# Key totals: a third accumulating fold to 16 rows, stacked half as wide, so that two squares a batch are turned and added in place of four

## The chip, the core and the metric

The kernel runs on one core of a Trainium2 chip. The core has five engines with a queue of instructions each: TensorE (PE in the profile, with its weight loads as PEld), VectorE (DVE), ScalarE (ACT), GpSimd (POOL) and SyncE (SP, which here only issues transfers). Each works through its queue in order, and engines wait for one another by semaphores. Transfers that SP and POOL issue are carried out by 16 DMA engines beside them. The metric is the time of one execution on the device in microseconds; lower is better.

## The reference

Input `x` has 32 images of 256 channels and 32 x 32 = 1024 positions. A group norm (32 groups of 8 channels) is followed by causal attention with eight heads of 32 channels, and `x` is added to the result. Cut to what matters here:

```python
q, k, v = heads(q_w @ xn + q_b), heads(kv_w @ xn + kv_b)      # 8 heads, 1024 positions, 32 channels
scores = q @ k.T / sqrt(32);  scores[query <= key] = -10000
attn = softmax(scores);       attn[query <= key] = 0
out = x + attn @ v
```

The softmax needs one total over the keys for each query. These totals, and how they are gathered, are what the change is about.

## The kernel before

**Layout.** A batch is one image. Scores are computed turned over: keys lie on the 128 partitions, queries along the rows. The exponentials of a block of scores are one tile `e` of 128 partitions x 4 heads x 512 queries, and TensorE multiplies it with `v` to the output `acc`. The total for a query is therefore a sum over partitions and over all tiles of keys. The kernel first adds the tiles to one another on VectorE (`add_keys`, line 469). What is left is called a square here: 128 partitions x 4 heads x 512 queries, four of them a batch (two groups `g` of four heads, two halves `hf` of the queries), numbered n = 0 to 3 in the code and called the first to the fourth.

**Loop.** The batches are cut into twelve visits each (`VISITS`, six for each group of heads). The loop at line 785 takes one visit after another, in this order: `scores` (products of queries and keys, exponentials on ScalarE, and on GpSimd in two visits of three the triangle mask of the blocks on the diagonal, `mask`, line 356), then the pieces of work that the dictionary `at` has for this visit, then `values` and `add_keys` of the visit before, then the pieces in `after`. All engines are scheduled by hand: what stands earlier in this order stands earlier in each engine's queue. `at` and `after` are filled at lines 739 to 784.

**From square to totals.** `fold(b, n, rows)` (line 478) has GpSimd issue an accumulating transfer that adds the partitions `rows` to `2 * rows` of a square to its first `rows` partitions. It runs with 64, then with 32; in front of the second square's second fold GpSimd drains. `stack` (line 484) has SyncE copy the 32 partitions that are left into the tile `folded`, each square at its own quarter of the partitions. When all four are there, `sum_folded` (line 490) goes through the four heads: VectorE turns 128 x 512 numbers in blocks of 32 x 32 and adds each row of 32, which leaves a query's total. `invert` takes the reciprocals, writes them to DRAM (line 536), and `spread_inverses` (line 545) reads them back to every channel's partition (`rb`); `finish` (line 568) multiplies, adds `x` and sends the result. The visits of a batch's folds are those of `SUMS = (3, 7, 10, 13)`, counted from the batch's first visit: those over 11 lie in the batch after.

**The group norm of the next batch** runs beside this. VectorE takes statistics (`norm_channels`), SyncE writes them to DRAM (`norm_gather`, line 198, tile `each`), GpSimd reads them back by groups (`norm_spread`, line 205, tile `eight`), VectorE aggregates them, GpSimd raises them to the power -1/2 and scales them (`norm_rstd`, lines 243 and 247, tiles `rstd` and `shift`), and ScalarE applies them (`norm_apply`, line 262, tile `xn`).

**The last batch** gets its totals from TensorE instead (`sums`, line 508, and `end_last`). It uses the same space: `rb_last` (line 557) and, in the very beginning, `less_mean` (line 706) lie in the tile tagged `folded`.

The lines that place the folds are these:

```python
v = first + SUMS[n]
late = int(n == 0)
when(v + 2 * late, lambda b=b, n=n: fold(b, n, 2 * HD), at if late else after)
when(v + 2 + late, lambda b=b, n=n: fold(b, n, HD), after)
when(v + 4, lambda b=b, n=n: stack(b, n), after if late else at)
```

Of the kernel before, what the change touches and what calls it, by code (L numbers as in the profile page):

```python
# [9 lines left out]
F32 = mybir.dt.float32  # L10
I32 = mybir.dt.int32
AF = mybir.ActivationFunctionType
ALU = mybir.AluOpType
# [4 lines left out]
P = 128  # L18
HD = 32
# [6 lines left out]
SUM_MAX = 1.0e20  # L26
HALFBANK = HALF // 2
ROW = 64
KEYS = 64


@with_exitstack
def tile_norm_attention_residual(
# [69 lines left out]
    def unshifted():  # L103
# [379 lines left out]

        def stack(b, n):
            if n == 0:
                live["folded", b] = work.tile([P, 4, HALF], F32, tag="folded", bufs=1, name=f"folded_{b}")
            total = live.pop(("sum", b, *divmod(n, NH)))
            nc.sync.dma_start(out=live["folded", b][n * HD : (n + 1) * HD], in_=total[:HD])

        def sum_folded(b, heads):  # L490
            if heads.start == 0:
                live["rows", b] = small.tile([P, ROW], F32, tag="rows", name=f"rows_{b}")
            for j in heads:
                turned = small.tile([P, HALF], F32, tag="turned", bufs=1, name=f"turned_{b}_{j}")
                nc.vector.transpose(turned, live["folded", b][:, j, :])
                nc.vector.tensor_reduce(
                    live["rows", b][:, j * HALF // HD : (j + 1) * HALF // HD],
                    turned.rearrange("p (k r) -> p k r", r=HD), AX.X, ALU.add,
                )

        def sum_keys(pd, e, of, start=True, stop=True):
            for j in range(4):
# [50 lines left out]
        def invert_here(b, n, within=slice(0, HALF)):  # L553


            if ("rb", b) not in live:
                live["rb", b] = work.tile([P, 4, HALF], F32, tag="folded", bufs=1, name="rb_last")
            k = (within.stop - within.start) // HD
            turned = small.tile([P, HALF], F32, tag="turned", bufs=1, name=f"turned_{b}_{n}_{within.start}")[:, : k * HD]
            nc.vector.transpose(turned, live["den", n][:, within])  # L560
            inv = inv_last[:, n, within.start // HD : within.stop // HD]
            nc.vector.reciprocal(inv, turned.rearrange("p (k r) -> p k r", r=HD)[:, :, 0])  # L562
            nc.vector.transpose(  # L563
                live["rb", b][:, n, within].rearrange("p (k r) -> p k r", r=HD),
                inv.unsqueeze(2).broadcast_to([P, k, HD]),
            )
# [124 lines left out]
        with tc.manual_schedule(engines={ENG.PE, ENG.Activation, ENG.DVE, ENG.Pool, ENG.SP}):  # L691
# [11 lines left out]
                norm_channels(0, g)  # L703
            norm_mean(0)
            keep_busy(2)
            odd = work.tile([P, 4, HALF], F32, tag="folded", bufs=1, name="less_mean")[:, 0, :]
            live["less_mean"] = odd.rearrange("p (g n t) -> p g n t", g=NG, t=P)
            for g in range(NG):
                nc.scalar.activation(
# [29 lines left out]
            for b in range(B):  # L739
# [14 lines left out]
                if not last:  # L754
                    for n in every:
                        v = first + SUMS[n]
                        late = int(n == 0)
                        when(v + 2 * late, lambda b=b, n=n: fold(b, n, 2 * HD), at if late else after)
                        when(v + 2 + late, lambda b=b, n=n: fold(b, n, HD), after)
                        when(v + 4, lambda b=b, n=n: stack(b, n), after if late else at)  # L760
                    late = b == B - 2
                    v = first + N + (5 if late else 6)
                    when(v, lambda b=b: sum_folded(b, every[:2]), after)
                    when(v + 1, lambda b=b: sum_folded(b, every[2:]), after)
                    when(v + 2, lambda b=b: invert(b))
                    for n in every:
                        at_visit = v + 2 + (0 if late else SPREAD[n])
                        if not late and n > 1:
                            when(at_visit, with_scores)
                        when(at_visit, lambda b=b, n=n: spread_inverses(b, n))  # L770
                    for n in every:
                        v = first + (N + 9 + n // 2 if late else FINISH[n])
                        later = None if late else lambda send, first=first, v=v, n=n: when(*((first + 2 * N + 4, send) if n < 2 else (v + 1, send, after)))
                        when(v, lambda b=b, n=n, later=later: finish(b, n, later=later), after)
                else:
                    when(first + 3, lambda: sums(0, SUMMED[1], False), after)
                    when(first + 7, lambda: sums(1, SUMMED[5], False), after)
                    when(first + 9, lambda: sums(2, SUMMED[7], False), after)
                    when(first + 8, lambda b=b: invert_here(b, 0))
                    when(first + 9, lambda b=b: finish(b, 0))  # L780
                    when(first + 8, lambda b=b: invert_here(b, 1))
                    when(first + 8, lambda b=b: finish(b, 1))
                    when(first + 10, lambda b=b: invert_here(b, 2))
                    when(first + 11, lambda b=b: finish(b, 2), after)
# [195 lines left out]
```

## Time and profile before

| what | value |
|---|---|
| time, median of 3 runs | 1791.73 us (1791.54 to 1792.0) |
| span of the profiled execution | 1791.2 us |
| PE busy | 1782.1 us, 99% |
| DVE busy | 1669.4 us, 93% |
| ACT busy | 1441.4 us, 80% |
| POOL busy | 897.9 us, 50% |
| mean busy share of the 16 DMA engines in the steady part | 0.70 |

The time of a run covers the span and what little lies around it; the profiled execution's own time isn't listed apart, and its span is 0.5 us below the median of the runs. The views used below are the page (totals of the span), the view by lines (groups of instructions of one kind, with their busy time, the mean of one, and the idle time before them), the view by windows (busy time of each engine in a stretch), the timeline of an engine (instructions in order of time, neighbours of one kind merged), and the view of DMA issues (size, and median time from issue to landing). A group's row reads: line, engine, operation, output <- inputs, shapes, count, then busy us and mean ns, then idle us of the engine before it and what ended that. Issuing a transfer from POOL counts as busy time of POOL, and the transfer itself goes on afterwards.

### The profile page before, as it was taken

The page shows a single profiled execution, that of the slowest core. Times are in us where ns is not written, and L with a number is a line of the kernel's source. Part 1 is how long each engine was busy: PE and PEld are TensorE (multiplying, and loading weights), DVE is VectorE, ACT ScalarE, POOL GpSimd, SP SyncE. Part 2 cuts the span into 40 slices and gives each one's busy share as a digit, 9 for nine tenths or more (in the row PEclk, how much of TensorE's full clock was granted, in tenths as well). Part 3 has the DMA queues.
Part 4 walks back from the last instruction along what each step waited for, and adds up shares of the span by engine and source line. Part 5 has one row for each costly group of instructions (what it writes and reads, how often), then busy time and mean ns, then how long its engine had stood idle before and what let it go on. Part 6 is the DMA issues. An engine that isn't in the chain of part 4 may idle for free.

```text
span 1791.2 us, 81784 instructions
## 1 busy us (share of the span) xinstructions
PE 1782.1 (99%) x37036; PEld 936.1 (52%) x37036; DVE 1669.4 (93%) x1796; ACT 1441.4 (80%) x1928; POOL 897.9 (50%) x935
## 2 busy tenths in 40 slices
PE   9999999999999999999999999999999999999998
PEld 5555555555555555555555555555555555555554
DVE  4689999999999999999999999999999999999998
ACT  6888878888778788788887888877888878888785
POOL 2355554554555555545555555454455554554542
PEclk9999999999999999999999999999999999999999
DMA  2567766767677676676776676767766766777663
GB/s 72 105 117 142 137 133 135 148 138 147 128 142 138 137 141 138 132 144 142 142 138 134 137 142 138 150 129 140 139 145 131 141 136 135 149 138 141 133 109 98
DMA packets 92771, 240.21 MB, mean 134 GB/s; under 512 B 26272, under 2 KB 27792, under 8 KB 76544
## 3 DMA queue, kind: packets, MB, share of 16 engines
q0 software_dynamic: 17360, 100.58, 40.1%
q1 hardware_dynamic: 74912, 134.28, 25.9%
q8 instruction: 290, 4.75, 1.1%
q14 instruction: 65, 0.53, 0.1%
q10 hardware_dynamic: 144, 0.07, 0.0%
HBM read 69.90 MB, written 34.95 MB: 59 GB/s over the span
## 4 chain that ended last, share of the span: by engine, by line
PE 99%; DVE 0%; ACT 0%; issue 0%; POOL 0%; POOLq 0%
PE sT L329 31%; PE acc L451 28%; PE pp L173 27%; PE ppv L173 13%; PE pd L503 1%; PE busy L159 0%; PE wt L152 0%; ACT e L426 0%; DVE rb_last L576 0%; DVE rb_last L563 0%; DVE turned L560 0%; DVE acc L573 0%; DVE inv_last L562 0%; POOL ident masks.py:199 0%; PE pv L173 0%
## 5 line engine op out<-in xcount | busy, mean ns | idle before, releaser
L426 ACT ACTIVATE e<-sT 128x1024 f32<-128x1024 f32 x768 | 744.3, 1022 | 301.5 <-PE sT L329 298.8
L366 POOL TENSOR_SCALAR_AFFINE_SELECT diagonal<-eh 128x512 f32<-128x512 f32 x512 | 563.3, 1122 | 625.4 <-ACT eh L422 624.7
L469 DVE TENSOR_TENSOR e<-e,e 128x1024 f32<-128x1024 f32 x314 | 578.0, 1841 | 23.0 <-ACT v L293 3.5
L329 PE MATMUL sT<-q,k 32*64 32x64 f32 (+1 forms) x18928 | 577.9, 367 | 0.1
L329 PEld LDWEIGHTS sT<-q,k 32*64 32x64 f32 x18928 | 397.0, 131 | 203.8 <-PE sT L329 67.4
L173 PE MATMUL pp<-xn,wT 128*32 128x512 f32 x4096 | 492.3, 598 | 0.0
L451 PE MATMUL acc<-e,v 128*32 128x512 f32 (+3 forms) x4608 | 401.0, 450 | 0.0
L422 ACT ACTIVATE eh<-sT 128x768 f32<-128x768 f32 (+1 forms) x384 | 341.6, 890 | 0.0
L451 PEld LDWEIGHTS acc<-e,v 128*32 128x32 f32 x4608 | 149.2, 110 | 261.5 <-issue 239.0
L173 PE MATMUL ppv<-wT,xn 128*32 128x256 f32 x4096 | 247.5, 382 | 0.0
L469 DVE TENSOR_TENSOR diagonal<-diagonal,e 128x1536 f32<-128x1536 f32 x126 | 194.5, 1544 | 16.1 <-PE acc L451 6.5
L173 PEld LDWEIGHTS pp<-xn,wT 128*32 128x32 f32 x4096 | 107.0, 109 | 195.8 <-issue 163.7
L469 DVE TENSOR_TENSOR e<-e,eh 128x1024 f32<-128x1024 f32 x126 | 177.6, 1410 | 6.5
L451 PEld LDWEIGHTS acc<-diagonal,v 128*32 128x32 f32 x4096 | 120.9, 110 | 88.1 <-issue 68.2
L173 PEld LDWEIGHTS ppv<-wT,xn 128*32 128x32 f32 x4096 | 120.2, 109 | 80.0 <-issue 7.0
L469 DVE TENSOR_TENSOR e<-e,diagonal 128x2048 f32<-128x2048 f32 x63 | 144.0, 2285 | 18.9 <-POOL diagonal L366 18.7
L451 PE MATMUL acc<-diagonal,v 128*32 128x128 f32 x4096 | 158.9, 273 | 0.0
L205 POOL DMA_INDIRECT eight<-each,group_of x31 | 42.9, 1383 | 193.4 <-DMA each<-st 193.4
L262 ACT ACTIVATE xn<-x,shift,rstd 128x256 f32<-128x256 f32 x248 | 137.2, 614 | 0.8 <-POOL shift L247 0.8
L576 DVE SCALAR_TENSOR_TENSOR rb<-num,v_bias_col,x 128x256 f32<-128x256 f32 x248 | 121.5, 530 | 4.4
L482 POOL DMA_DIRECT2D e<-e x124 | 103.6, 835 | 42.6 <-issue 42.6
L482 POOL DMA_DIRECT2D diagonal<-diagonal x124 | 105.1, 847 | 0.7
(87 smaller groups left out, 1092.2 us busy)
## 6 DMA issues: line engine op xcount, KB each, us to landing
x<-in_x_dram SPq DMA_DIRECT2D x124, 256.0 KB, 3.8
diagonal<-diagonal POOLq DMA_DIRECT2D x62, 512.0 KB, 6.1
e<-e POOLq DMA_DIRECT2D x62, 512.0 KB, 5.7
rb<-inverses SPq DMA_DIRECT2D x124, 256.0 KB, 4.0
out_dram<-rb SPq DMA_DIRECT2D x124, 256.0 KB, 4.2
diagonal<-diagonal POOLq DMA_DIRECT2D x62, 256.0 KB, 4.6
folded<-diagonal SPq DMA_DIRECT2D x62, 256.0 KB, 5.1
e<-e POOLq DMA_DIRECT2D x62, 256.0 KB, 4.6
```

Of the source, the lines that this page charges most:

```text
L173: nc.tensor.matmul(out[part], lhsT=lhsT[:, part], rhs=rhs, start=start, stop=stop, skip_group_check=True)
L205: nc.gpsimd.indirect_dma_start(eight, None, live["each", b].rearrange("(m c) s -> m (c s)", c=CPG), bass.IndirectOffsetOnAxis(ap=group_of[ ...
L262: nc.scalar.activation(to, of, AF.Identity, bias=live["shift", b][:, g : g + 1], scale=rstd)
L329: return nc.tensor.matmul(bank[c : c + KEYS, cols], lhsT=live["k", b, g][rows, kb * P + c : kb * P + c + KEYS], rhs=live["q", b, g][rows, ...
L366: nc.gpsimd.affine_select(out=square[:, :, place + s * P : place + (s + 1) * P], in_=raw[:, :, (1 - s) * KEYS : (3 - s) * KEYS], pattern=[ ...
L422: exp = nc.scalar.activation(eh.rearrange("p (n bank) q -> p bank n q", n=2)[:, :, :, :narrow], short[:, :, :, :narrow], AF.Exp)
L426: nc.scalar.activation(e[:, 2 * a : 2 * a + 2, :wide], pairs[a][:, :, :wide], AF.Exp)
L451: nc.tensor.matmul(acc[HD * j : HD * (j + 1), of], lhsT=live["v", b][:, kb, h * HD : (h + 1) * HD], rhs=e[:, j, :], start=first, stop=last ...
L469: nc.vector.tensor_add(to, to, tile_of(b, g, at))
L482: nc.gpsimd.dma_start(out=total[:rows], in_=total[rows : 2 * rows], accum_op=ALU.add)
L503: nc.tensor.matmul(pd[HD * j : HD * (j + 1), of], lhsT=pick, rhs=e[:, j, :], start=start, stop=stop, skip_group_check=True,)
L576: nc.vector.scalar_tensor_tensor(blocks(rb, s), blocks(num, s, (start + s) % 2 == 1), v_bias_col[:, g : g + 1], blocks(xt[:, g, cols], s), ...
```

## The change

The second fold is followed by a third, from 32 to 16 partitions (`TURN`), and each now comes one visit after the one before (with the first square one visit later than that, as before). `stack` copies 16 partitions in two halves of 256 queries, each half to 16 partitions of its own, so that `folded` has the same 128 partitions and half the columns. `sum_folded` turns two heads at once, 128 x 512 numbers, and adds rows of 16. The first square's `stack` comes one visit later. The tile is now tagged `stacked`; `rb_last` takes a slot of the pool of the images instead, and `less_mean` the narrower tile.

```diff
+TURN = 16
...
             if n == 0:
-                live["folded", b] = work.tile([P, 4, HALF], F32, tag="folded", bufs=1, name=f"folded_{b}")
+                live["folded", b] = work.tile([P, 4, HALFBANK], F32, tag="stacked", bufs=1, name=f"folded_{b}")
             total = live.pop(("sum", b, *divmod(n, NH)))
-            nc.sync.dma_start(out=live["folded", b][n * HD : (n + 1) * HD], in_=total[:HD])
+            for s in range(2):
+                at = n * HD + s * TURN
+                nc.sync.dma_start(
+                    out=live["folded", b][at : at + TURN], in_=total[:TURN, :, s * HALFBANK : (s + 1) * HALFBANK]
+                )
...
-            for j in heads:
-                turned = small.tile([P, HALF], F32, tag="turned", bufs=1, name=f"turned_{b}_{j}")
-                nc.vector.transpose(turned, live["folded", b][:, j, :])
-                nc.vector.tensor_reduce(
-                    live["rows", b][:, j * HALF // HD : (j + 1) * HALF // HD],
-                    turned.rearrange("p (k r) -> p k r", r=HD), AX.X, ALU.add,
-                )
+            turned = small.tile([P, HALF], F32, tag="turned", bufs=1, name=f"turned_{b}_{heads.start}")
+            nc.vector.transpose(turned, live["folded", b][:, heads.start : heads.stop, :].rearrange("p j q -> p (j q)"))
+            nc.vector.tensor_reduce(
+                live["rows", b].rearrange("p (j s k) -> p j k s", s=2, k=HALFBANK // HD)[:, heads.start : heads.stop],
+                turned.rearrange("p (j k s r) -> p j k s r", j=len(heads), s=2, r=TURN), AX.X, ALU.add,
+            )
...
-                live["rb", b] = work.tile([P, 4, HALF], F32, tag="folded", bufs=1, name="rb_last")
+                live["rb", b] = xpool.tile([P, NG, S], F32, tag="x", name="rb_last").rearrange("p g (hf q) -> p (g hf) q", hf=NH)
...
                         when(v + 2 * late, lambda b=b, n=n: fold(b, n, 2 * HD), at if late else after)
-                        when(v + 2 + late, lambda b=b, n=n: fold(b, n, HD), after)
-                        when(v + 4, lambda b=b, n=n: stack(b, n), after if late else at)
+                        when(v + 1 + 2 * late, lambda b=b, n=n: fold(b, n, HD), after)
+                        when(v + 2 + 2 * late, lambda b=b, n=n: fold(b, n, TURN), after)
+                        when(v + 4 + late, lambda b=b, n=n: stack(b, n), after if late else at)
```

## What was predicted

> **What bounds the kernel now.** The page comes first: span, busy line, granted clock.
>
> ```profile
> span 1791.2 us, 81784 instructions
> PE 1782.1 (99%) x37036; PEld 936.1 (52%) x37036; DVE 1669.4 (93%) x1796; ACT 1441.4 (80%) x1928; POOL 897.9 (50%) x935
> PEclk9999999999999999999999999999999999999999
> ```
>
> PE is never idle and has the full clock. DVE, the engine that the change relieves, is second at 93%. Whether PE's pace depends on DVE is read from three batches in the view by windows (columns: stretch, its length, then busy us of PE, PEld, DVE, ACT, POOL, then clock, DMA share, GB/s).
>
> ```profile
> 70.35:125.33 54.98, 54.98 (x1161) 28.86 (x1159) 45.41 (x43) 44.99 (x61) 26.12 (x30) 1.00 0.60 110
> 125.33:180.31 54.98, 54.98 (x1161) 28.86 (x1159) 51.61 (x56) 44.94 (x61) 26.81 (x29) 1.00 0.70 139
> 845.00:899.98 54.98, 54.98 (x1166) 28.86 (x1155) 52.70 (x57) 44.94 (x60) 28.55 (x29) 1.00 0.70 139
> ```
>
> The batch takes 54.98 us with 45.41 us of DVE work in it and with 52.70. DVE has nothing to give to the end time. What is left to ask is whether the change makes somebody else late for PE, and by the edit that is POOL, whose queue carries the accumulating transfers. Here is POOL's timeline for one steady batch (start, duration, engine, line, operation, tiles, and in brackets what it idled for). L366 is the triangle mask that PE's value products read, L482 an accumulating transfer, L205 the gather of the group norm of the batch after, L243 its power.
>
> ```profile
> 842.24 0.85 POOL L482 DMA_DIRECT2D diagonal<-diagonal  x1
> 848.16 2.24 POOL L366 TENSOR_SCALAR_AFFINE_SELECT diagonal<-eh 128x512 f32<-128x512 f32 x2 [5.07 <-ACT eh L422]
> ...
> 850.39 0.80 POOL L482 DMA_DIRECT2D diagonal<-diagonal  x1
> 852.75 1.66 POOL L366 TENSOR_SCALAR_AFFINE_SELECT diagonal<-eh 128x512 f32<-128x512 f32 x2 [1.56 <-ACT eh L422]
> 854.37 0.84 POOL L482 DMA_DIRECT2D e<-e  x1
> 861.49 1.28 POOL L205 DMA_INDIRECT eight<-each,group_of  x1 [6.29 <-DMA each<-st]
> 862.78 2.37 POOL L366 TENSOR_SCALAR_AFFINE_SELECT diagonal<-eh 128x512 f32<-128x512 f32 x2
> 865.11 0.85 POOL L482 DMA_DIRECT2D e<-e  x1
> 866.46 1.22 POOL L366 TENSOR_SCALAR_AFFINE_SELECT diagonal<-eh 128x512 f32<-128x512 f32 x2 [0.50 <-ACT eh L422]
> 867.85 2.69 POOL L243 TENSOR_TENSOR rstd<-rstd,power 128x2 f32<-128x2 f32 x1 [0.18 <-DVE rstd L217]
> ...
> 870.84 0.91 POOL L482 DMA_DIRECT2D diagonal<-diagonal  x1
> ...
> 878.68 0.82 POOL L482 DMA_DIRECT2D diagonal<-diagonal  x1
> ...
> 881.78 0.84 POOL L482 DMA_DIRECT2D e<-e  x1
> 888.98 2.81 POOL L366 TENSOR_SCALAR_AFFINE_SELECT diagonal<-eh 128x512 f32<-128x512 f32 x2 [6.36 <-ACT eh L422]
> 893.13 0.82 POOL L482 DMA_DIRECT2D e<-e  x1 [1.33 <-issue]
> 893.97 3.29 POOL L366 TENSOR_SCALAR_AFFINE_SELECT diagonal<-eh 128x512 f32<-128x512 f32 x2
> 897.21 0.85 POOL L482 DMA_DIRECT2D diagonal<-diagonal  x1
> ```
>
> Two things are to be seen. No transfer here waits for the one before it to land: the second fold of a square comes 7.8 us or more after the first. And the queue is in order: the gather idles 6.29 us for its input, and the mask behind it starts only at 862.78, when the gather is done. PE reads that mask, and the one of 888.98, here:
>
> ```profile
> 866.55 0.62 PE L451 MATMUL acc<-diagonal,v 128*32 128x128 f32 x16
> ...
> 894.04 0.62 PE L451 MATMUL acc<-diagonal,v 128*32 128x128 f32 x16
> ```
>
> The first mask ends at 865.15, so it has 1.4 us in hand; the second at 891.79, 2.2 us in hand.
>
> **The change, part by part.** DVE's part, from the view by line and shape:
>
> ```profile
> L495 DVE STREAM_TRANSPOSE turned<-folded 128x512 f32<-128x512 f32 x124 | 87.8, 708 | 2.2
> L496 DVE TENSOR_REDUCE rows<-turned 128x16 f32<-128x512 f32 x124 | 85.0, 686 | 4.3
> ```
>
> A batch loses four transposes and four sums, 4 x (0.708 + 0.686) = 5.6 us, and gets two of each, over the same 512 columns: 2.8 us. DVE goes from 52.7 to about 49.9 us of 54.98. A sum with 32 outputs in a four-step pattern isn't in the trace: I take 0.69 us, and at twice that DVE still does less than now. Worth to the span: 0, by the windows above. The one stall of PE that DVE causes in the whole trace bounds the gain: a DVE sum that took 2.50 us for its usual 1.41 (rows of the DVE and PE timelines), and later a block of scores of 2.25 us that is elsewhere 1.55.
>
> ```profile
> 605.06 2.50 DVE L469 TENSOR_TENSOR e<-e,eh 128x1024 f32<-128x1024 f32 x1
> ...
> 618.82 2.25 PE L329 MATMUL sT<-q,k 32*64 32x256 f32 x48
> ```
>
> That costs PE 0.7 us, once. The new places of `rb_last` and `less_mean` cost nothing: the slot in `xpool` was batch 28's, long finished, and the other is a smaller tile of the same lifetime.
>
> The transfers are what matters. A square gets a third fold, so POOL issues 12 a batch, not 8 (4 x 0.84 = 3.4 us more of a half idle engine: hidden if nothing waits). But the folds now follow each other one visit apart, 54.98 / 12 = 4.58 us, and each reads what the last one wrote. How long they take to land is in the DMA view (KB, us from issue to landing):
>
> ```profile
> diagonal<-diagonal POOLq DMA_DIRECT2D x62, 512.0 KB, 6.1
> e<-e POOLq DMA_DIRECT2D x62, 512.0 KB, 5.7
> diagonal<-diagonal POOLq DMA_DIRECT2D x62, 256.0 KB, 4.6
> ...
> e<-e POOLq DMA_DIRECT2D x62, 256.0 KB, 4.6
> ...
> each<-st SPq DMA_DIRECT2D x31, 12.0 KB, 5.3
> ```
>
> 6.1, 5.7 and 4.6 us are over 4.58: nearly every second and third fold will stop POOL's queue until the one before has landed, with masks, gather and power behind it (the first square's second fold keeps its old distance and waits only when the queue is late already). SP's queue has the same: `stack` of the third square stands ahead of the statistics that the gather waits for.
>
> ```profile
> 855.26 0.51 SPq L488 DMA_DIRECT2D folded<-diagonal  x1
> 855.87 1.56 SPq L198 DMA_DIRECT2D each<-st  x1
> ```
>
> It is issued when the last fold has landed (850.39 + 4.6 = 855.0 now), and is two issues instead of one. The 16-row fold isn't in the trace. From 512 to 256 KB the landing falls by 1.1 to 1.5 us, so another 128 KB less should take 0.55 to 0.75 off 4.6: I take 4.0 us. Its bounds are 4.6 us and, by the fastest `stack`, 2.9 us:
>
> ```profile
> DMA to landing us min/median/max: 2.9/4.9/7.0
> ```
>
> The waits now close into a ring, once round per batch, each step being queued behind or reading the one before. From the first fold of the third square: it lands 6.1; second fold lands 4.6; third 4.0; two stack issues 1.0; statistics land 5.3; gather 0.3 after that (861.49 against 855.87 + 5.3) and 1.3 long; mask 2.24; fold 0.85; mask 2.24; power and shift to the next transfer 3.0 (870.84 less 867.85); first square 6.1 and 4.6; its third issue 0.84; second square 5.7 and 4.6; its third issue 0.84; mask 2.24; and the third square is due again. The 2.24 is twice the mean of one select:
>
> ```profile
> L366 POOL TENSOR_SCALAR_AFFINE_SELECT diagonal<-eh 128x512 f32<-128x512 f32 x512 | 563.3, 1122 | 625.4 <-ACT eh L422 624.7
> ```
>
> The sum is 55.85 us. PE's batch is 54.98, so POOL's ring is 0.87 us longer and becomes the period. Followed by the clock it says the same: third fold at 842.24 + 10.7 = 852.9, landed 856.9, statistics issued at 858.0 instead of 855.87, so the mask of 862.78 starts 2.1 us late and has 1.4 us in hand: PE stalls 0.7 us. The ring is complete in batches 1 to 30, 30 times: 30 x 0.87 = 26 us. From the span, 1791.2 + 26 = 1817.2; the runs' median is 0.5 above the span, so **1817.7 us**.
>
> The drain ahead of the second square's second fold (the 1.33 us before 893.13) moves under the wait for the landing: 0.
>
> [...]
>
> **Bounds of the unknowns.** The 16-row fold: -1.1 to +0.6 us. Masks range from 1.22 to 3.29 us in the rows above, so the ring's three make -3.1 to +3.2. The second square's first fold (881.78) now takes 7.9 us:
>
> ```profile
> DMA to landing us min/median/max: 7.9/7.9/7.9
> ```
>
> Issued 2.3 us later, clear of most of the x loads, I take the median 5.7; up to +2.2 if not. Below a ring of 54.98 nothing happens; with masks at mean and 7.9 it is 58.05, 3.1 us a batch.
>
> **The rivals.**
> No change. The ring closes inside 54.98, for which 0.9 us of the three masks is enough (one as short as the 1.22 us row), and the masks' own 1.4 and 2.2 us in hand take the rest. DVE's 2.8 us of extra idle time per batch speaks for it, the in-order gather row and the 0.87 us against it. Time: 1791.7, give or take 1.5. This is the side on which the forecast would be wrong. If the change doesn't do what it says (a reduction as slow as the two it replaces), DVE's share comes out as before, and by the windows the time is the same as in this case.
> Much slower. The second square's fold still takes 7.9 us, POOL's shift comes late for ACT's normalisation too, and the ring is 3.1 us over: 1791.7 + 92 = 1884. For it: four transfers in flight around that moment. Against: their order changes.
> Faster. DVE would have to be on PE's path somewhere. It was once, for 0.7 us: 1791.0. A gain above 0.2% (3.6 us, about what a measurement of this kernel can tell from no change) has no place in the trace.
>
> **Chances.** Stall of some tenths to 2.5 us a batch, the forecast: 0.53. No change: 0.33. Much slower: 0.12. Faster by over 0.2%: 0.02. So faster 0.02, same 0.33, slower 0.65. The range goes from 1789 (no change at its lower end) to 1868 (2.5 us a batch, half way between the median ring and the long one with a little over), which leaves out most of the much slower case.
>
> **What would show it.** Right: in the windows of a batch, 55.3 to 57.5 us for the same 1160 or so matmuls; POOL's second and third folds with idle time before them, ended by a DMA; waits of PE or its loads for the masks; statistics issued some 2 us later within the batch. DVE at about 50 us a batch either way. Wrong: batches of 54.98 us with POOL waiting on landings all the same (then the masks had enough in hand), or folds that land within 4.58 us and don't wait. If batches are long but PE's blocks wait for ACT or DVE, the place is wrong and only the sign right.

## The result, and the profile after

The changed kernel takes 1968.16 us (median of four runs, 1966.90 to 1974.57) beside 1791.87 us for the kernel before in the same session (1791.54 to 1794.06): ratio 1.0989, with a 95% interval of 1.0972 to 1.1007. It is slower by 176.3 us, or 5.9 us for each of 30 batches. The forecast had the sign and the place, and was 150 us short. An experiment without a range below was timed once; repeated runs of the kernel before lie within 0.4% of one another.

All line numbers move up a little: the fold is L483 now, the mask L367, the gather L206, power L244, `stack` L491, the transposes L499 and the sums L500. From the page: span, busy times, and the shares of the chain of work that ended last.

```profile
span 1965.4 us, 82254 instructions
PE 1861.8 (95%) x37036; PEld 938.3 (48%) x37036; DVE 1595.1 (81%) x1672; ACT 1440.3 (73%) x1928; POOL 877.7 (45%) x1059
...
DMA 35%; PE 18%; POOL 16%; issue 13%; DVE 11%; ACT 5%; SPq 0%; POOLq 0%; DVEq 0%; ACTq 0%
```

PE, which was idle for 9 us, is now idle for 104, and a third of the chain is transfers that somebody waits for. PE's busy time has also grown by 80 us, with the same 37036 matmuls: at most 29 of these are a lowered clock (last section), and where the others come from was not followed up. No other engine has become busier to speak of; the rest is waiting. The view of waits names them (engine, tile and line, what was waited for: us in all, times, longest):

```profile
POOL diagonal L483 <- DMA diagonal<-diagonal: 352.2, 99, 6.9
POOL e L483 <- DMA e<-e: 280.5, 83, 6.8
...
POOL e L483 <- issue: 231.1, 33, 8.3
DVE e L470 <- POOL diagonal L367: 200.7, 32, 8.3
PEld acc L452 <- POOL diagonal L367: 158.9, 153, 3.9
POOL diagonal L367 <- ACT eh L423: 122.8, 44, 9.0
...
PE acc L452 <- POOL diagonal L367: 80.5, 90, 3.0
```

GpSimd spends 352.2 + 280.5 us before a fold, until the transfer before has landed. The 231.1 us of "issue" are the drain ahead of the second square's second fold (experiment `e3_no_drain` shows that). The idle time that GpSimd had before, 624.7 us of waiting for ScalarE's exponentials ahead of a mask, has shrunk to 122.8: its slack is used up, and now DVE, PE and PE's loads wait for the masks. One stretch of GpSimd's timeline has it in order:

```profile
890.20 0.92 POOL L483 DMA_DIRECT2D diagonal<-diagonal  x1 [0.33 <-PE sT L330]
893.60 4.15 POOL L367 TENSOR_SCALAR_AFFINE_SELECT diagonal<-eh 128x512 f32<-128x512 f32 x2 [2.48 <-ACT eh L423]
...
897.74 0.83 POOL L483 DMA_DIRECT2D diagonal<-diagonal  x1
898.29 1.52 POOL L367 TENSOR_SCALAR_AFFINE_SELECT diagonal<-eh 128x512 f32<-128x512 f32 x2
902.64 0.81 POOL L483 DMA_DIRECT2D diagonal<-diagonal  x1 [2.83 <-DMA diagonal<-diagonal]
903.25 1.06 POOL L483 DMA_DIRECT2D e<-e  x1
912.50 0.76 POOL L483 DMA_DIRECT2D e<-e  x1 [8.19 <-issue]
913.02 1.48 POOL L367 TENSOR_SCALAR_AFFINE_SELECT diagonal<-eh 128x512 f32<-128x512 f32 x2
917.84 0.81 POOL L483 DMA_DIRECT2D e<-e  x1 [3.33 <-DMA e<-e]
```

The first square's third fold (902.64) idles 2.83 us for its second. The second square's first fold is issued at 903.25, its second only at 912.50 after 8.19 us of idle time, and behind that stands the mask of 913.02. PE's timeline shows who needs it:

```profile
910.75 1.04 PE L452 MATMUL acc<-e,v 128*32 128x512 f32 x8
913.98 0.43 PE L452 MATMUL acc<-diagonal,v 128*32 128x128 f32 x8 [2.19 <-POOL diagonal L367]
```

The view of DMA issues (KB each, median us to landing) gives the sizes that the forecast had to estimate:

```profile
diagonal<-diagonal POOLq DMA_DIRECT2D x62, 512.0 KB, 6.5
e<-e POOLq DMA_DIRECT2D x62, 512.0 KB, 7.0
...
diagonal<-diagonal POOLq DMA_DIRECT2D x62, 256.0 KB, 4.7
e<-e POOLq DMA_DIRECT2D x62, 256.0 KB, 5.0
diagonal<-diagonal POOLq DMA_DIRECT2D x62, 128.0 KB, 4.2
...
e<-e POOLq DMA_DIRECT2D x62, 128.0 KB, 4.2
```

The forecast's ring can be measured link by link: the mean time from one of GpSimd's transfers (or the power) to the next, worked out from the trace over 22 steady batches, with the mean landing time of the first of the two beside it. In the kernel before the same count gives a period of 55.02 us.

```
link in GpSimd's queue (after)                  us   lands after
3rd square, first fold  -> second              6.67   6.37
3rd square, second fold -> third               5.01   4.70
3rd, third fold -> 4th square, first           1.73   4.14
4th square, first fold  -> second              6.36   6.08
4th square, second fold -> gather              1.60
gather -> 4th square, third fold               3.88
4th, third fold -> power                       3.30
power -> 1st square, first fold                3.31
1st square, first fold  -> second              7.67   7.14
1st square, second fold -> third               5.15   4.89
1st, third fold -> 2nd square, first           0.61   4.20
2nd square, first fold  -> second (drain)      8.71   7.67
2nd square, second fold -> third               5.26   4.96
2nd, third fold -> 3rd square, first           1.70   4.15
period                                        60.96
```

60.96 is 5.98 us over PE's 54.98; 30 of those are 179 us, against 176.3 measured. In 6 of the 14 links the next step comes about 0.3 us after a landing (1.04 behind the drain): these end in waits for a landing. Together they last 37.2 us of the 61. A seventh, the first square's first fold, has landed 0.5 us before the next step, which in most batches starts when the masks ahead of it end.

The ring is not closed by GpSimd alone. Between the gather and the power it runs through the gather's landing (5.6 us by the view of DMA issues, 3.0 before) and VectorE's aggregation, and the power waits for that in every batch:

```profile
DVE mv L213 <- DMA eight<-each,group_of: 81.9, 24, 5.0
...
POOL rstd L244 <- DVE rstd L218: 34.8, 31, 2.4
```

### The profile page after: what moved, and what is told of

Read it like the earlier page. It is cut to its first block, busy times and chain, and to the rows that moved or that the text cites. A ratio compares the mean times of both kernels' runs of the same rounds, so it can differ in the third digit from the quotient of the medians.

```text
span 1965.4 us, 82254 instructions
## 1 busy us (share of the span) xinstructions
PE 1861.8 (95%) x37036; PEld 938.3 (48%) x37036; DVE 1595.1 (81%) x1672; ACT 1440.3 (73%) x1928; POOL 877.7 (45%) x1059
## 4 chain that ended last, share of the span: by engine, by line
DMA 35%; PE 18%; POOL 16%; issue 13%; DVE 11%; ACT 5%; SPq 0%; POOLq 0%; DVEq 0%; ACTq 0%
DMA e<-e 19%; POOL diagonal L367 9%; DMA eight<-each,group_of 7%; PE sT L330 6%; DMA diagonal<-diagonal 6%; PE acc L452 5%; DVE e L470 4%; POOL rstd L244 4%; PE pp L174 4%; ACT e L427 3%; PE ppv L174 3%; DMA each<-st 2%; POOL diagonal L483 2%; DVE mv L213 2%; DVE st L190 1%
## 5 line engine op out<-in xcount | busy, mean ns | idle before, releaser
L330 PE MATMUL sT<-q,k 32*64 32x64 f32 (+1 forms) x18928 | 612.1, 375 | 3.8 <-ACT e L427 3.3
L367 POOL TENSOR_SCALAR_AFFINE_SELECT diagonal<-eh 128x512 f32<-128x512 f32 x512 | 481.0, 1047 | 123.0 <-ACT eh L423 122.8
L330 PEld LDWEIGHTS sT<-q,k 32*64 32x64 f32 x18928 | 411.6, 133 | 219.2 <-PE sT L330 61.0
L483 POOL DMA_DIRECT2D e<-e x186 | 167.7, 902 | 512.0 <-DMA e<-e 280.5
L483 POOL DMA_DIRECT2D diagonal<-diagonal x186 | 164.7, 886 | 362.2 <-DMA diagonal<-diagonal 352.2
L452 PE MATMUL acc<-diagonal,v 128*32 128x128 f32 x4096 | 178.2, 280 | 91.1 <-POOL diagonal L367 80.5
L174 PE MATMUL ppv<-wT,xn 128*32 128x256 f32 x4096 | 254.7, 389 | 0.0
L452 PEld LDWEIGHTS acc<-diagonal,v 128*32 128x32 f32 x4096 | 108.5, 110 | 222.8 <-POOL diagonal L367 158.9
L470 DVE TENSOR_TENSOR e<-e,eh 128x1024 f32<-128x1024 f32 x126 | 201.7, 1601 | 6.5
L244 POOL TENSOR_TENSOR rstd<-rstd,power 128x2 f32<-128x2 f32 x32 | 82.4, 2574 | 41.7 <-DVE rstd L218 34.8
```

The source lines that it names most:

```text
L174: nc.tensor.matmul(out[part], lhsT=lhsT[:, part], rhs=rhs, start=start, stop=stop, skip_group_check=True)
L244: nc.gpsimd.tensor_tensor(rstd, rstd, power, ALU.pow)
L330: return nc.tensor.matmul(bank[c : c + KEYS, cols], lhsT=live["k", b, g][rows, kb * P + c : kb * P + c + KEYS], rhs=live["q", b, g][rows, ...
L367: nc.gpsimd.affine_select(out=square[:, :, place + s * P : place + (s + 1) * P], in_=raw[:, :, (1 - s) * KEYS : (3 - s) * KEYS], pattern=[ ...
L452: nc.tensor.matmul(acc[HD * j : HD * (j + 1), of], lhsT=live["v", b][:, kb, h * HD : (h + 1) * HD], rhs=e[:, j, :], start=first, stop=last ...
L470: nc.vector.tensor_add(to, to, tile_of(b, g, at))
```

## The experiments

The theory to be tested: the period is set by GpSimd's queue, since each third fold waits there for the second one's landing, and the second for the first's. The rivals: the load of four more transfers a batch; the closer spacing alone; the drain; the path through `stack` and the statistics; and some cost of the narrower stack itself.

**The narrower stack and DVE's relief alone** (`e8_half_stack_alone`). The third fold is left out and the other folds and `stack` stand where they stood before, so each total lacks its partitions 16 to 31.

```diff
-                        when(v + 1 + 2 * late, lambda b=b, n=n: fold(b, n, HD), after)
-                        when(v + 2 + 2 * late, lambda b=b, n=n: fold(b, n, TURN), after)
-                        when(v + 4 + late, lambda b=b, n=n: stack(b, n), after if late else at)
+                        when(v + 2 + late, lambda b=b, n=n: fold(b, n, HD), after)
+                        when(v + 4, lambda b=b, n=n: stack(b, n), after if late else at)
```

> The changed kernel without the third fold, the first two folds and the stack at the visits of before. It leaves out half of each total (rows 16 to 31 of each square), so what is added up is not complete; stack in two halves, half as many squares turned and added, are as in the change. Theory (VectorE is off PE's path, eight small stack issues for four large ones are hidden): 1790 to 1793 us with VectorE some 2.8 us a batch less busy. Rival (the two halves of a stack cost SP or the DMA engines what PE then waits for): 1800 us or more. Rival (VectorE's relief is worth something that the third folds hide): under 1788 us.

It took 1792.00 us (1790.86 to 1792.66), ratio 0.9994, interval 0.9984 to 1.0004. A batch in the view by windows (busy us of PE, PEld, DVE, ACT, POOL):

```profile
845.00:899.98 54.98, 54.93 (x1158) 28.59 (x1149) 48.02 (x52) 44.83 (x60) 29.51 (x29) 1.00 0.64 123
```

DVE has the relief, and the batch still takes 54.98 us. What the change was to bring is worth nothing here, and the two half stacks cost nothing: all 176 us belong to the folds.

**The closer spacing alone** (`e1_spacing_only`): the kernel before, its second fold one visit after the first.

```diff
-                        when(v + 2 + late, lambda b=b, n=n: fold(b, n, HD), after)
+                        when(v + 1 + 2 * late, lambda b=b, n=n: fold(b, n, HD), after)
```

> The kernel before, with one edit: each square's second fold comes one visit after its first, as in the change. No third fold, no half-wide stack. Theory (a ring of waits on landings in GpSimd's in-order queue, closed once per batch): without the third folds the ring of the changed kernel loses 4.2 us (third square's landing), 4.9 + 0.6 less 1.9 us (first square), 5.3 + 0.5 + 1.2 less 3.5 us (second square) and some 1.4 us of the second stack issue, about 47 us in all, under 54.98, so it doesn't set the period; what can still be late is the mask behind the second square's second fold, by 0 to 0.5 us a batch: 1792 to 1806 us. Rival (the second folds' shorter distance is the harm, the third fold is only more of the same): at least half of the loss, 1875 us or more. Rival (the loss is DMA contention or the half-wide stack, not any wait in the queue): 1791 to 1793 us.

1807.20 us, 15 us more than before (1792.10) and 1 us past the upper end. Its waits:

```profile
POOL e L482 <- DMA e<-e: 395.7, 62, 10.4
...
POOL diagonal L482 <- DMA diagonal<-diagonal: 166.3, 31, 6.9
```

562 us of waiting on landings cost 15: two folds a square in a row still fit into GpSimd's slack, nearly.

**The third fold, with the first two at their old distance** (`e2_third_only`).

```diff
-                        when(v + 1 + 2 * late, lambda b=b, n=n: fold(b, n, HD), after)
-                        when(v + 2 + 2 * late, lambda b=b, n=n: fold(b, n, TURN), after)
+                        when(v + 2 + late, lambda b=b, n=n: fold(b, n, HD), after)
+                        when(v + 3 + late, lambda b=b, n=n: fold(b, n, TURN), after)
```

> The changed kernel with the first two folds of each square at the visits of before, and the third fold one visit after the second. Stack, turning and adding as in the change. Theory (ring of waits): the second folds no longer wait, the third ones still do, since a second fold takes 4.6 to 5.3 us and a visit is 4.58: the third square's third fold stands ahead of the fourth square's first one and of the stack that the statistics wait behind, and the fourth square's third fold stands ahead of the power. Mask after the gather late by some 2 us, shift late by 3 us: 2 to 4 us a batch, 1850 to 1910 us. Rival (only the shortened distance of the second folds matters): 1791 to 1800 us. Rival (contention and smaller packets of the added transfers, wherever they are placed): 1940 us or more.

1933.09 us: above the range. Only 35 us come back, though GpSimd waits far less for landings, 306 us in place of 633:

```profile
POOL e L483 <- DMA e<-e: 153.8, 58, 3.8
POOL diagonal L483 <- DMA diagonal<-diagonal: 152.5, 72, 3.4
```

So the sum of GpSimd's waits doesn't price them (562 us cost 15 in `e1_spacing_only`). What counts, by the theory, is whether the ring still closes in time: counted as above, it takes 59.7 us here. Which of its links made it longer than expected was not worked out.

**The same transfers without the wait** (`e9_third_aside`), the test that decides between wait and load. The third fold is issued at its place, with its 128 KB (as 32 rows of 4 KB, where the change has 16 rows of 8 KB), but adds a tile of zeros to itself, which nobody reads. The addition of partitions 16 to 31 is left out; `stack`, too, then waits for the second fold only.

```diff
+    aside = const.tile([P, 4, HALFBANK], F32, name="aside")
+    nc.gpsimd.memset(aside[: 2 * HD], 0.0)
...
+            if rows == TURN:
+                total, rows = aside, HD
```

> The changed kernel, its third folds at their places in GpSimd's queue, but adding 128 KB of a tile of zeros to itself (32 rows of 4 KB), so that they don't read what the second fold writes and have nothing to wait for. It leaves out the third sixteen rows' addition of each total. Transfers, bytes, stacks, VectorE work and queue order are those of the change. Theory (what costs is the queue standing still until the second fold has landed): the ring is open, what is left is what the shorter distance of the second folds costs (1807 us measured without third folds): 1800 to 1825 us. Rival (12 accumulating transfers a batch load the DMA engines or GpSimd so much that all land late): 1930 us or more. Between the two, the share of each.

1809.88 us, as expected. Its waits, and its row of the third folds in the view of DMA issues:

```profile
POOL e L487 <- issue: 239.8, 40, 8.8
POOL diagonal L369 <- ACT eh L425: 228.7, 119, 8.5
POOL diagonal L487 <- DMA diagonal<-diagonal: 180.7, 31, 6.6
POOL e L487 <- DMA e<-e: 163.4, 32, 7.6
```

```profile
aside<-aside POOLq DMA_DIRECT2D x124, 128.0 KB, 4.9
```

As many transfers of as many bytes in the same order, and 158 us of the 176 are gone. The second folds still wait for landings (180.7 and 163.4), and the drain is as long as ever; together with the added transfers they account for no more than the 17 us that are left. The earlier start of the stacks isn't what helps: in the changed kernel no engine waits for a stack to land, and the statistics, which queue behind the third square's stack, go ahead of it in `e5_stack_behind` (below) without any gain. The period of the ring, counted as above, is 55.6 us.

**The same at the places of `e2_third_only`** (`e10_third_aside_old_places`): the edit of `e9_third_aside`, with the same addition left out, and the two lines of `e2_third_only`.

> As the run before it, with the second folds at the visits of the kernel before, two visits after the first, and the third folds (of the zeros, leaving out the same part) one visit after those, as in the run with the third fold alone, which took 1933 us. Theory: nothing in GpSimd's queue waits for a landing any more: 1790 to 1796 us with the same 12 transfers a batch. Rival (the load of the transfers): 1900 us or more.

1811.24 us (1808.72 to 1813.48), ratio 1.0099, interval 1.0082 to 1.0116: the forecast of no change is missed by 15 us. So four more transfers a batch do cost something, about 1%, without anybody waiting for them; whether by their load on the DMA engines or by the time that GpSimd needs to issue them was not separated. Landings:

```profile
diagonal<-diagonal POOLq DMA_DIRECT2D x62, 512.0 KB, 6.8
e<-e POOLq DMA_DIRECT2D x62, 512.0 KB, 7.4
```

The first folds land at 6.8 and 7.4 us, in place of 6.1 and 5.7 before. Against `e2_third_only`, which has the same places and the wait, it is 122 us less: again the wait is the bulk. With `e9_third_aside` the parts are not additive: closer spacing alone is 15 us, the four transfers alone 19, both together 17.

**The drain** (`e3_no_drain`).

```diff
-            if (n, rows) == (1, HD):
-                nc.gpsimd.drain()
```

> The changed kernel without the drain of GpSimd ahead of the second square's second fold. Its trace has that fold starting 1.07 us after its predecessor's landing, where other folds start 0.28 us after. Theory (ring of waits, with the drain as one of its links): 0.8 us a batch less, 24 us, 1944 us (1935 to 1953). Rival (the drain is what makes the queue wait for landings, as its length of 8.8 us in the trace could suggest): the loss falls by half or more, under 1880 us. Rival (the drain is outside whatever sets the period): 1965 to 1971 us.

1972.64 us, no gain where 1944 was expected. The "issue" row of 231.1 us is gone, and its time stands with the landing instead (280.5 us before):

```profile
POOL e L481 <- DMA e<-e: 506.1, 114, 8.0
```

That link of the ring gets 0.65 us shorter (8.71 to 8.06), and the next one 0.92 longer (5.26 to 6.18): given back.

**The place of `stack`** (`e5_stack_behind`): the third square's stack behind the statistics in SP's queue.

```diff
-                        when(v + 4 + late, lambda b=b, n=n: stack(b, n), after if late else at)
+                        when(v + 4 + late + int(n == 2), lambda b=b, n=n: stack(b, n), after if late else at)
```

> The changed kernel with the third square's stack one visit later, so that it stands behind the statistics' transfer on SyncE, not ahead of it. Theory (ring of waits): statistics, gather and mask no longer wait for the third square's third fold, but the queue still goes on through the fourth square's first fold, whose second fold stands ahead of the gather: from the third fold's start to the gather it is 8.5 us in place of 9.5, so about 1 us a batch less: 1935 to 1950 us. Rival (SyncE's order is the main cause): under 1880 us. Rival (GpSimd's queue alone sets the period): 1965 to 1971 us.

1966.84 us: no gain, as the rival said (GpSimd's queue alone sets the period). The forecast's ring went through this stack and the statistics. In the changed kernel the gather does wait for the statistics in 22 batches, for 29.8 us in all, but without that wait (8.8 us are left of it here) the ring is as long through GpSimd's folds.

**The image loads beside the second square** (`e4_load_later`): `LOAD = 7` becomes `LOAD = 10`, so that the four loads of `x` are issued elsewhere.

> The changed kernel with the image's four loads three visits later (10 for 7). In its trace the second square's first fold, queued among these loads, landed after 8.2 us, other first folds after 5.8. Theory (ring of waits, this landing one of its links): up to 2.4 us a batch less, 72 us, 1896 us, less what the loads give to the transfers they stand beside now: 1890 to 1945 us. Rival (the landing doesn't set the period): 1960 to 1972 us.

2013.11 us: worse, where 1890 to 1945 was expected. The second square's first fold still lands after 7.67 us on average, so these loads are not what holds it; and its second fold now lands after 6.66 us in place of 4.96. In the view of DMA issues the folds of both `e` squares together:

```profile
e<-e POOLq DMA_DIRECT2D x62, 512.0 KB, 7.0
...
e<-e POOLq DMA_DIRECT2D x62, 256.0 KB, 5.4
```

**Another order of the two squares** (`e11_swap`): the first square's third fold and its stack one visit later, so that the second square's first fold needn't stand behind a landing.

```diff
-                        when(v + 2 + 2 * late, lambda b=b, n=n: fold(b, n, TURN), after)
-                        when(v + 4 + late, lambda b=b, n=n: stack(b, n), after if late else at)
+                        when(v + 2 + 3 * late, lambda b=b, n=n: fold(b, n, TURN), after)
+                        when(v + 4 + 2 * late, lambda b=b, n=n: stack(b, n), after if late else at)
```

> The changed kernel with the first square's third fold and its stack one visit later, so that the second square's first fold goes ahead of it. All results complete. In the changed kernel's ring the wait for the first square's second fold to land stands between (5.15 us and 0.6 us of issue); with the swap the second square's fold is due some 1.9 us after the first square's second one. Theory: the ring is 3.8 us shorter, 57.1 us: 1791 + 30 x 2.1 = 1855 us, up to 1890 us if later landings stretch as they did when the drain was taken out. Rival (no single link matters, since the others take the time up again): 1940 to 1975 us.

1942.97 us, where the rival was right and the theory's 1855 to 1890 too bold. The period is 60.1 us: the first square's third fold, now issued 1.7 us behind the second square's first fold, lands after 6.8 us in place of 4.2, and the second square's third fold comes 5.90 us after its second.

**Two visits between folds** (`e6_two_visits`, `e7_two_visits_mended`): can the third fold be had for nothing? The first:

```diff
-        SPREAD = (2, 2, 4, 5)
+        SPREAD = (1, 1, 3, 4)
...
-                        when(v + 1 + 2 * late, lambda b=b, n=n: fold(b, n, HD), after)
-                        when(v + 2 + 2 * late, lambda b=b, n=n: fold(b, n, TURN), after)
-                        when(v + 4 + late, lambda b=b, n=n: stack(b, n), after if late else at)
+                        when(v + 2 + late, lambda b=b, n=n: fold(b, n, HD), after)
+                        when(v + 4 + late, lambda b=b, n=n: fold(b, n, TURN), after)
+                        when(v + 5 + 2 * late, lambda b=b, n=n: stack(b, n))
...
-                    v = first + N + (5 if late else 6)
+                    v = first + N + (6 if late else 7)
```

> The changed kernel with two visits between one fold of a square and the next, as between the two folds of before, the stacks one visit later and all issued ahead of the values, and the turning one visit later. The same number of transfers, instructions and bytes as the changed kernel: only places in the queues differ. Theory (ring of waits): no fold finds the one before it still in flight, so nothing is queued behind a landing; POOL has 3.4 us more of issuing in a batch and is half idle: 1790 to 1797 us, batches of 54.98 us. Rival (the number of transfers, their contention, or the half-wide stack costs the time): still over 1900 us. Rival (part queue, part contention): 1800 to 1880 us.

1926.98 us (1913.83 to 1937.13), ratio 1.0756, interval 1.0694 to 1.0818: far from the 1790 to 1797 expected. GpSimd hardly waits for landings any more (34.1 and 31.6 us, where the change has 280.5 and 352.2), and somebody else waits:

```profile
ACT e L427 <- DMA folded<-e: 115.9, 33, 4.6
...
POOL e L483 <- DMA e<-e: 34.1, 22, 2.9
POOL diagonal L483 <- DMA diagonal<-diagonal: 31.6, 42, 1.5
```

ScalarE can't write the next exponentials, since the tile of a square, mostly the fourth, is still being read by its stack. The wait has moved from GpSimd to ScalarE. The second version has the old `SPREAD` and place of `sum_folded`, and takes the fourth square's third fold and stack earlier:

```diff
+                        when(v + 2 + late, lambda b=b, n=n: fold(b, n, HD), after)
+                        when(v + 4 + late, lambda b=b, n=n: fold(b, n, TURN), at if n == 3 else after)
+                        when(v + (7, 5, 5, 4)[n], lambda b=b, n=n: stack(b, n))
```

> As the run with two visits between folds, with its new wait taken away: there ScalarE waited 115.9 us for the fourth square's stack to land, because its tile is written again three visits after that stack. Here the fourth square's third fold is issued ahead of the next batch's first fold and its stack at the visit of before; the other stacks come when their third fold has landed, the third square's behind the group norm's statistics. All transfers, bytes and VectorE work of the changed kernel are there. Theory (only queued-up waits cost time): 1790 to 1797 us. Rival (more and smaller transfers cost time by contention wherever they stand): 1830 us or more.

Missed as well: the four runs took 1816.32, 1868.67, 1869.18 and 1874.74 us, all of them above the kernel before. The profile is that of the 1869.18 us, and says nothing of the shortest. In it 13 of the 31 batches last 55.0 us to the tenth, as wanted, but six last 61 to 67:

```
length of the batches, us, in order (e7_two_visits_mended)
55.0 55.0 55.0 55.2 56.7 62.6 55.9 55.0 55.0 55.0 55.0 55.0 66.6 58.2 55.5 66.8
58.4 67.3 55.3 64.6 55.0 57.8 56.8 55.0 56.3 55.3 61.0 56.3 55.0 55.0 55.0
```

Both waits are still in its view:

```profile
POOL diagonal L483 <- DMA diagonal<-diagonal: 130.7, 73, 4.3
...
POOL e L483 <- DMA e<-e: 74.3, 29, 4.6
ACT e L427 <- DMA folded<-e: 70.4, 11, 11.6
```

Eleven of them, up to 11.6 us long, stop ScalarE. The schedule fits in some batches and not in others, and what tips single batches over is not settled. The shortest run of any version with a third fold in the chain is this one's 1816.32 us, 1.3% above the kernel before (1792.42), and by `e8_half_stack_alone` there would be nothing to win.

## Why the prediction was right and wrong, by its own steps

**Right.** That PE's 54.98 us a batch are the bound and DVE's relief is worth nothing (`e8_half_stack_alone`, 0.9994 of the time before); that a 16-row fold lands in about 4.0 us (4.2); that second and third folds wait for landings in GpSimd's queue, that this closes a ring and that the ring becomes the period (`e9_third_aside`: without the third folds' wait, 158 us less). PE waits for masks, as the last part said.

**Wrong: the ring's length.** 0.87 us over 54.98 were forecast, and 5.98 measured. The sum of 55.85 us was only 8% short of 60.96, but the forecast is the small difference of two large numbers, and that was short by a factor of 7. By terms:

```
term of the predicted ring                        predicted   measured
3rd square's first and second fold, landed          10.70      11.68
its third fold to the gather                        10.60       9.69
gather, mask, fold, mask, power and shift            9.63      10.49
1st square's folds to the third's issue             11.54      13.43
2nd square's folds, the third's issue, mask         13.38      15.67
sum                                                 55.85      60.96
```

- *The second square's first fold* was taken at 5.7 us, with a bound of 7.9 from the kernel before. It lands after 7.67, and the drain adds 1.04 behind the landing: 8.71, or 3.0 us over, the largest single term. "Clear of most of the x loads" was the reason for 5.7; `e4_load_later` shows that these loads aren't what makes it long.
- *The drain* was costed at 0, "under the wait for the landing". It ends 1 us after the landing. Taking it out gave nothing (`e3_no_drain`), so this error alone didn't cost the forecast anything; but the link was mis-sized by it.
- *The first square's first fold* was taken at 6.1 and takes 7.67: it lands after 7.14, and in the stretch shown above the second fold, at 897.74, stands behind a pair of masks that waited for ScalarE and ended then. The prediction's own rows have 7.84 us between these two folds (870.84 to 878.68), and it says that this distance stays; its sum took the landing in place of it.
- *Landings as such* were taken from the kernel before. With four more transfers a batch the 512 KB rows go from 6.1 and 5.7 to 6.5 and 7.0 us, and `e10_third_aside_old_places` shows such longer landings where nobody waits for the new ones.
- *From landing to the next issue* no time was allowed. It is about 0.3 us, at each of the links that wait.
- *The third fold to the gather* was led through `stack` and the statistics (10.6). In the trace the gather stands behind the fourth square's first fold and its landing (1.73 + 6.36 + 1.60 = 9.69), and moving the stack changed nothing (`e5_stack_behind`).
- *The gather to the power* was priced as GpSimd's own work, 1.3 + 2.24 + 0.85 + 2.24 = 6.63 us. It takes 3.88 + 3.30 = 7.18: the power waits for VectorE behind the gather's landing, a wait that the sum had at nothing.
- *The masks* were taken at 2.24 us a pair in series. A pair is shorter on average in the changed kernel (2 x 1.047 us, below), so this error went the other way.

**The range.** The text had bounds for the 16-row fold (+0.6), the masks (+3.2) and the second square's fold (+2.2). All three at their upper ends make 55.85 + 6.0 = 61.85, 6.9 us a batch, 206 us. The range stopped at 2.5 us a batch, which left the upper ends out; with a ring that is hardly longer than PE's batch, every term at its upper end is worth 30 times itself.

**The rival "much slower"** had the right condition (7.9 us for the second square's fold), a right companion (POOL's shift late for ScalarE's normalisation, a wait that took 0.8 us before):

```profile
ACT xn L263 <- POOL shift L248: 56.5, 29, 3.4
```

and half the price, 92 us, because it changed one term and left the others at their medians from a trace without the ring.

## What to carry to other kernels

In the changed kernel, a transfer that waited for an earlier one's landing held up what stood behind it in GpSimd's queue (the mask of 913.02 stood behind a second fold that had idled for 8.19 us); before adding one to a chain, add up the whole round of that queue, with landings at their upper ends, and compare it with the period. Where the sum comes near the period, the forecast is a difference of two large numbers, and its range is that of all terms together. And an engine at 93% beside one at 99% is by itself no reason for a trade: here the relief was worth nothing (`e8_half_stack_alone`, 0.9994 of the time before), and was paid for with the slack of a half idle queue.

## What the runs showed of the hardware that was not expected

- **A quarter of the bytes took some six tenths of the time.** In the changed kernel the accumulating transfers of 512, 256 and 128 KB land after 6.5 to 7.0, 4.7 to 5.0 and 4.2 us.
- **PE lost half its clock behind 16 of 33 stalls.** The view by windows around the stall of 911 to 914, with the granted clock third from last:

```profile
911.00:915.00 4.00, 1.66 (x32) 0.40 (x29) 2.16 (x1) 1.02 (x2) 2.00 (x3) 1.00 0.69 151
...
915.50:916.00 0.50, 0.50 (x24) 0.31 (x16) 0.00 (x0) 0.00 (x0) 0.00 (x0) 0.74 1.33 164
916.00:919.00 3.00, 3.00 (x44) 1.48 (x32) 0.00 (x0) 2.76 (x3) 1.16 (x3) 0.50 0.09 14
919.00:919.50 0.50, 0.50 (x12) 0.27 (x8) 0.00 (x0) 0.10 (x1) 0.50 (x2) 0.84 2.13 197
919.50:925.00 5.50, 5.50 (x126) 2.67 (x117) 4.86 (x3) 3.21 (x5) 1.22 (x2) 1.00 0.72 120
```

  PE waits 2.19 us, works on at full clock for some 1.8 us, then has half of it for 3.4 us (the three rows below 1.00 lose 0.13 + 1.50 + 0.08 = 1.71 us of clock, as much as 3.4 us at half do), and has it back by 919.2. Summed over windows of 2 us this is 29 us of lost clock in the changed kernel from 60 to 1900 us, and none in the kernel before up to 1750 us or in `e9_third_aside` up to 1770 us. PE's weight loads waited 3.10 us in this stall. Between 30 and 1905 us the trace has 33 gaps of PE of over 1 us, none over 3.1 us long, and the clock fell within 1.8 us behind 16 of them, to half each time: for 3.41 us behind 15 of them, for 6.83 us behind one. Gaps of 1.91 us are among those 16 and among the other 17, so their length alone doesn't decide it. Of the 176 us the lost clock makes at most 29 directly. `e11_swap` has lost less of it (a mean granted clock of 0.994 over the span, 0.985 in the changed kernel) and is still 150 us slower than the kernel before.
- **The masks are shorter in the changed kernel.** Over the whole kernel the mean of one select falls from 1122 to 1047 ns:

```profile
L367 POOL TENSOR_SCALAR_AFFINE_SELECT diagonal<-eh 128x512 f32<-128x512 f32 x512 | 481.0, 1047 | 123.0 <-ACT eh L423 122.8
```

  Why was not found. By the traces, selects that ran wholly beside an idle VectorE took 0.85 us on average in the changed kernel (142 of them), and those that ran wholly beside a busy one got shorter too, from 1.12 us (166 of them) to 0.94 (185).

- **A link made shorter was given back elsewhere.** Without the drain one link lost 0.65 us and the next gained 0.92 (`e3_no_drain`). In `e11_swap` the ring was to lose 3.8 us and lost 0.9, as the first square's third fold, now in flight beside the second square's first one, landed 2.6 us later. Why it lands later is not shown.

Open are two things. The second square's first fold lands, on average, after 7.9 us in the kernel before, some 7.7 in the changed one and in `e9_third_aside`, 7.4 in `e1_spacing_only` and `e8_half_stack_alone`, and 7.1 in `e11_swap`; why it takes longer than the others, apart from the image loads, was not found. And why `e7_two_visits_mended` drops out of step in some batches wasn't tried.
